# Transposing on the tensor engine instead of by DMA in an attention block between two feed-forward halves

## The chip, the core and the metric

The kernel runs on one core of a Trainium2 chip. The metric is device time in microseconds (us) of one execution of the whole program. Five engines work side by side, each through its own in-order queue: PE (matrix multiplication), DVE (vector), ACT (activation functions and copies), POOL (general) and SP, which here only issues DMAs. SBUF is the on-chip memory that all of them read; PE writes its results to PSUM, whose banks hold 512 32-bit or 1024 16-bit numbers for each of 128 partitions.

## The reference

The input is `(2, 1024, 1024)` in 32-bit floats: two sequences of 1024 tokens, width 1024.

```
x = x + 0.5 * ffn(layernorm(x))
x = x + attention(layernorm(x))
x = x + 0.5 * ffn(layernorm(x))
```

- `ffn(y) = y @ base_w.T + base_b + 2 * sum over the top 2 of 8 experts of weight * (y @ A_e.T) @ B_e`, the experts being adapters of rank 16, with a softmax over the two best gate logits.
- `attention`: 32 query heads in 8 groups of 4 that share a key and value head, head width 32, rotary positions on queries and keys, causal mask, softmax, output projection.

## The kernel before

Tokens are worked in 16 tiles of 128 (`t`); a tile goes through the stages `a1` (first layer norm and feed-forward), `a2` (second layer norm's result times the key/value and query weights, rotary), attention, `c1` (output projection and third layer norm) and `c2` (second feed-forward). Every large product is made of three 16-bit products, high x high, high x low and low x high, so each left operand is kept as a high and a low half and must lie with its columns on the partitions, that is, transposed, in a tile `tt` of 2 x 8 blocks of 128 x 128.

Transposition happens in three places.

1. Behind each layer norm (`layernorm`, 48 in all). `Split.add` makes the high half on ACT (L329) and the low half on DVE (L330) into `hl`, and a DMA transposition on SP's queue (L333) turns both into `tt`. For the first layer norm of the first three tiles (`turn=t < NTURN`) `turn_rows` transposes the 32-bit rows on PE instead (L365) and splits them from PSUM (L367, L368).
2. Keys (`kv_out`, L548): the staged keys `kst`, 8 groups of 128 columns (three parts of 32 and the rows for maxima), are turned by one DMA into `kts`.
3. Queries (`qt_load`, L625): two head groups at a time are turned by one DMA from `qst` into a tile `qt`.

Attention of a tile and a head group goes in two passes. `unit_s1` multiplies queries and keys (L645, four matmuls of 128 columns to a bank of the pool `p_s1`, which has three), and DVE takes the row maxima (L662; on the diagonal block after ACT's copy L656 and POOL's mask L657, in tiles with more than two key blocks). The maxima have to enter the second pass as extra rows of the queries. In tiles with up to three key blocks (`L <= MPE`) PE turns them (`turn_maxima`, L692) and DVE spreads them into the query tile (L694); in the others they are written into `qst` and the queries are turned again with them by a second DMA (L682, L683, then `qt_load`). `unit_s2` multiplies keys and queries (L796, one matmul of 512 columns), ACT takes the exponential (L802), and `av_batch` multiplies with values and ones (L739) after DVE's pair sums (L718).

The order is written out by hand. Attention units run along in a fixed order, first passes some units ahead of second passes (`look`, `LOOK`); between two steps of a second pass `step` takes pieces of dense work (`chunks`) from the list that `plan` gives for that tile, a few steps behind (`behind`). The program's scheduler then orders each engine's instructions. The weights of `a2` and `c1` do not fit in SBUF and are streamed: `prefetch` (L416) puts a load of 1 MB on SP's queue as soon as one of three buffers is free. Stores of results (L832, L834) and loads of `x` (L142) are on SP's queue too, in program order with the transpositions. One tile, `LATE`, is parked in DRAM (`xlate`, `qlate`) and taken up last.

Of the kernel before, what the change touches and what calls it, by code (L numbers as in the profile page):

```python
# [9 lines left out]
FP = mybir.dt.float32  # L10
# [24 lines left out]
LOFF = 2  # L35
MPE = 3
NTURN = 3
SB, LB = 3, 2
# [3 lines left out]
def kernel(  # L42
# [76 lines left out]
    qst = [stat.tile([P, NH, P], HP, name=f"qst{j}") for j in range(2)]  # L119
    ksts = [stat.tile([P, NKV, P], HP, name=f"kst{j}") for j in range(2)]  # L120
    kts = stat.tile([P, TPB + 1, NKV, P], HP)
    wss = [stat.tile([P, 2, KB // 2, 512], HP, name=f"ws{j}") for j in range(3)]
    for kst in ksts:
        nc.gpsimd.memset(kst[:, :, MR : MR + MC], -MROW)
        nc.gpsimd.memset(kst[:, :, MR + MC :], 0.0)
    mms = stat.tile([P, MR + MC], HP, name="mm")
    nc.gpsimd.memset(mms, 0.0)

# [25 lines left out]
    S, INV = {}, {}  # L154
    stream = deque()
    stage_ctx = ExitStack()
    stg = stage_ctx.enter_context(tc.tile_pool(name="stg", bufs=1))
# [135 lines left out]
    def prep_rest():  # L293
        yield from prep_stream(2, (0, 1), [(1, 0, 0), (1, 1, 1)], True)
        yield from prep_stream(3, (2, 3), [(4, 0, 2), (4, 1, 5)], False)
        yield from prep_stream(0, (2, 0), [None, None], True)
        for j in range(2):
            nc.gpsimd.memset(qst[j][:, :, 3 * DH :], 0.0)
        yield from prep_stream(1, (1, 2), [None, None], True)
        yield from prep_stream(4, (0, 1), [None, None], False)  # L300
# [14 lines left out]

    class Split:


        def __init__(self, n):
            self.hl = hlp.tile([P, 2 * D], HP, name="hl")  # L320
            self.tt = tp.tile([P, 2 * KB, P], HP, name="tt")
            self.n, self.done = n, 0

        def add(self, src):

            w, i = D // self.n, self.done
            src = src[:, i * w : (i + 1) * w]
            hi = self.hl[:, 2 * i * w : (2 * i + 1) * w]
            nc.scalar.copy(hi, src)  # L329
            nc.vector.tensor_tensor(self.hl[:, (2 * i + 1) * w : (2 * i + 2) * w], src, hi, ALU.subtract)  # L330
            m = 2 * KB // self.n
            pin(
                nc.sync.dma_start_transpose(  # L333
                    out=self.tt[:, i * m : (i + 1) * m, :], in_=self.hl[:, 2 * i * w : (2 * i + 2) * w]
                )
            )
            self.done += 1

        def high(self, k):
            m = KB // self.n  # L340
            return self.tt[:, k // m * 2 * m + k % m, :]

        def low(self, k):
            m = KB // self.n
            return self.tt[:, k // m * 2 * m + m + k % m, :]

    class Halves:


        def __init__(self):  # L350
            self.tt = tp.tile([P, 2 * KB, P], HP, name="tt")

        def high(self, k):
            return self.tt[:, k, :]

        def low(self, k):
            return self.tt[:, KB + k, :]

    def turn_rows(xn):
# [10 lines left out]

    def layernorm(xt, n=1, turn=False):
        st = small.tile([P, 2, 6], FP, name="bst")
        for c in range(2):
            nc.vector.bn_stats(st[:, c, :], xt[:, bass.ts(c, 512)])  # L374
        mv = small.tile([P, 2], FP, name="mv")
        nc.vector.bn_aggr(mv, st.rearrange("p a b -> p (a b)"))
        ve = small.tile([P, 1], FP, name="ve")
        nc.gpsimd.tensor_scalar(ve, mv[:, 1:2], EPS, None, ALU.add)
        r = small.tile([P, 1], FP, name="r")
        nc.gpsimd.tensor_tensor(r, ve, mhalf, ALU.pow)  # L380
        n1 = small.tile([P, 1], FP, name="n1")
        nc.vector.scalar_tensor_tensor(n1, ve, r, r, ALU.mult, ALU.mult)
        nc.vector.tensor_scalar(n1, n1, -0.5 * XS, 1.5 * XS, ALU.mult, ALU.add)
        rs = small.tile([P, 1], FP, name="rs")
        nc.vector.tensor_tensor(rs, n1, r, ALU.mult)
        nb = small.tile([P, 1], FP, name="nb")
        nc.vector.scalar_tensor_tensor(nb, mv[:, 0:1], -1.0, rs, ALU.mult, ALU.mult)
        xn = fpool.tile([P, D], FP, name="xn")
        if turn:
            nc.scalar.activation(xn, xt, AF.Identity, bias=nb, scale=rs)  # L390
            return turn_rows(xn)
        sp = Split(n)
        for i in range(n):
            c = bass.ts(i, D // n)
            nc.scalar.activation(xn[:, c], xt[:, c], AF.Identity, bias=nb, scale=rs)
            sp.add(xn)
        return sp

    def dense(ps, tt, wsel, n=512, last=True):

        for k in range(KB):
            wh, wl = wsel(k)
            th, tl = tt.high(k), tt.low(k)
            nc.tensor.matmul(ps, lhsT=th, rhs=wh, start=(k == 0), stop=False)  # L404
            nc.tensor.matmul(ps, lhsT=th, rhs=wl, start=False, stop=False)  # L405
            nc.tensor.matmul(ps, lhsT=tl, rhs=wh, start=False, stop=(last and k == KB - 1))  # L406
            if k % 2 == 1:
                yield
# [87 lines left out]
    def stage_a1(t):  # L496
# [3 lines left out]
        def done(n):  # L500
            if n == 1:
                Ts["x2", t] = layernorm(xts[t])
                if t == LATE:
                    late["x"] = dram.tile([P, D], FP, name="xlate")
                    nc.sync.dma_start(out=late["x"], in_=xts.pop(t))
# [29 lines left out]
    def kv_out(t, ps):  # L535
# [11 lines left out]
        kt = kts[:, (t + TPB) % (TPB + 1)]  # L547
        nc.sync.dma_start_transpose(out=kt, in_=ks.rearrange("p g c -> p (g c)"))  # L548
        KT[t] = kt

    def q_out(t, n, ps):
# [7 lines left out]
        if t == LATE and n == 1:  # L559
            late["q"] = dram.tile([P, NH, P], HP, name="qlate")  # L560
            nc.sync.dma_start(out=late["q"], in_=qs)

# [11 lines left out]
    def stage_a2x(t):  # L574

        ts = (t, t + 1)
        tts = [Ts.pop(("x2", u)) for u in ts]
        for ci in (2, 0, 1):
            pss = [p_dense.tile([P, 512], FP, name="pd") for u in ts]
# [19 lines left out]
    def first_a2(ts):  # L599

        tts = [Ts.pop(("x2", t)) for t in ts]
        for ci in (2, 0, 1):
            pss = [p_dense.tile([P, 512], FP, name="pd") for t in ts]
# [17 lines left out]
    def qt_load(t, g):  # L621

        assert ready[t] == 2 or g * GRP < NH // 2
        q = qtp.tile([P, 2 * GRP, P], HP, name="qt")
        nc.sync.dma_start_transpose(  # L625
            out=q, in_=QS[t][:, g * GRP : (g + 2) * GRP, :].rearrange("p h c -> p (h c)")
        )
        return q

    def unit_s1(t, g):  # L630
# [4 lines left out]
        if not odd:  # L635
            Ts["mx"] = small.tile([P, 2, TPB, GRP], FP, name="mx", bufs=2)
        mx = Ts["mx"]
        q = Ts["q1", (t, g - odd)][:, odd * GRP : (odd + 1) * GRP, :]
        for j in reversed(range(L)):
# [23 lines left out]
            if turned:  # L663
                turn_maxima()
            yield
# [6 lines left out]
        else:  # L672
            m = mx[:, :, 0, :]
        if L <= MPE:
            mm = mms[:, MR:].rearrange("p (i a h) -> p i a h", i=2, a=2)
            nc.vector.tensor_scalar(mm[:, 0], m, 1.0 / MROW, None, ALU.mult)
            nc.vector.scalar_tensor_tensor(mm[:, 1], m, 1.0 / MROW, mm[:, 0], ALU.mult, ALU.subtract)
            turned.append((t, g - 1, q1))
            return
        qs = QS[t][:, (g - 1) * GRP : (g + 1) * GRP].rearrange("p (a h) c -> p a h c", a=2)  # L680
        mh, ml = qs[:, :, :, 3 * DH], qs[:, :, :, 3 * DH + 1]
        nc.vector.tensor_scalar(mh, m, 1.0 / MROW, None, ALU.mult)  # L682
        nc.vector.scalar_tensor_tensor(ml, m, 1.0 / MROW, mh, ALU.mult, ALU.subtract)  # L683
        Ts["q2", t, g - 1] = qt_load(t, g - 1)

    turned = deque()

    def turn_maxima():

        t, g, q1 = turned.popleft()  # L690
        ps = p_s1.tile([P, GRP, P], FP, name="s1")[:, 0, :]
        nc.tensor.matmul(ps[0 : MR + MC], lhsT=mms, rhs=ident16, start=True, stop=True)  # L692
        rows, heads = slice(MR, MR + MC), [MC, 2 * GRP, P]
# [92 lines left out]
    def unit_s2(t, g):  # L786
# [7 lines left out]
        for j in range(L):  # L794
            ps = p_s2.tile([P, GRP, P], FP, name="s2")
            ins = nc.tensor.matmul(  # L796
                ps.rearrange("p h k -> p (h k)"), lhsT=KT[b0 + j][:, g, :],
                rhs=q.rearrange("p h k -> p (h k)"), start=True, stop=True,
            )
# [3 lines left out]
            if j == L - 1:  # L803
# [3 lines left out]
                )  # L807
            av_add(t, g, j, L, p32)
            yield

# [102 lines left out]
    for t in START:  # L913
        if t == "f":
# [4 lines left out]
            continue  # L919
        for _ in chunk(a1[t]):  # L920
            if len(stream) < 3:
                next(pr, None)
# [6 lines left out]

    qtp = ctx.enter_context(tc.tile_pool(name="qt", bufs=5, reuse_waits="tile"))  # L930
    pp = ctx.enter_context(tc.tile_pool(name="pp", bufs=2, reuse_waits="tile"))
# [85 lines left out]
    def step(s):  # L1017
# [28 lines left out]
        for g in range(NKV):  # L1046
# [3 lines left out]
            if s == NT - 1 and g == 3:  # L1050
                QS[LATE] = qst[LATE % 2]
                nc.sync.dma_start(out=QS[LATE], in_=late["q"])
            if u < len(units) and units[u][0] != t and s < NT - 1:
# [85 lines left out]
```

## Time and profile before

| | |
|---|---|
| median of 3 runs | 1512.1 us (1508.58 to 1515.14) |
| profiled execution: time, span | 1510.2 us, 1508.5 us |
| mean granted clock of PE | 0.978 |
| PE busy | 1407.3 us, 93% of the span |
| DVE, ACT, POOL busy | 1136.9, 749.4, 388.6 us |
| DMA | 269.40 MB in 265266 packets, 227472 of them under 512 B |
| DMA transpositions: layer norms, queries, keys | 45, 104, 16; median from issue to landing 6.1, 3.5, 5.6 us |

Busy time is time in which at least one instruction of the engine ran. A matmul's row shows its whole passage through the array, so that neighbours overlap: two matmuls of 512 columns, 0.38 us each, start 0.215 us apart. What one costs in a row of many is read from start to start. The granted clock is the share of full speed that the chip gave PE.

### The profile page before, as it was taken

The page shows a single profiled execution, that of the slowest core. Times are in us where ns is not written, and L with a number is a line of the kernel's source. Part 1 is how long each engine was busy: PE and PEld are TensorE (multiplying, and loading weights), DVE is VectorE, ACT ScalarE, POOL GpSimd, SP SyncE. Part 2 cuts the span into 40 slices and gives each one's busy share as a digit, 9 for nine tenths or more (in the row PEclk, how much of TensorE's full clock was granted, in tenths as well). Part 3 has the DMA queues.
Part 4 walks back from the last instruction along what each step waited for, and adds up shares of the span by engine and source line. Part 5 has one row for each costly group of instructions (what it writes and reads, how often), then busy time and mean ns, then how long its engine had stood idle before and what let it go on. Part 6 is the DMA issues. An engine that isn't in the chain of part 4 may idle for free.

```text
span 1508.5 us, 35338 instructions
## 1 busy us (share of the span) xinstructions
PE 1407.3 (93%) x14596; PEld 787.6 (52%) x14596; DVE 1136.9 (75%) x2411; ACT 749.4 (50%) x1356; POOL 388.6 (26%) x642
## 2 busy tenths in 40 slices
PE   5877889989999999999999898999999999989998
PEld 3333445545555555565654454555555556556544
DVE  6876957777869789688863687886869689789753
ACT  8563435444545455465561334553645456556531
POOL 3442224222322222222120133322322122221120
PEclk9998999999999999999999899999999999999999
DMA  8989187468487874846658858669595863923552
GB/s 294 324 193 245 24 214 192 141 166 261 90 285 87 237 186 85 258 114 141 192 145 269 181 185 239 188 162 264 105 297 78 242 162 87 275 82 86 127 163 76
DMA packets 265266, 269.40 MB, mean 179 GB/s; under 512 B 227472, under 2 KB 230544, under 8 KB 245392
## 3 DMA queue, kind: packets, MB, share of 16 engines
q1 hardware_dynamic: 259024, 239.87, 57.3%
q0 software_dynamic: 4640, 16.78, 6.5%
q10 hardware_dynamic: 1440, 10.49, 1.9%
q8 instruction: 114, 1.87, 0.5%
q14 instruction: 48, 0.39, 0.1%
HBM read 191.60 MB, written 20.45 MB: 141 GB/s over the span
## 4 chain that ended last, share of the span: by engine, by line
PE 68%; DVE 13%; DMA 10%; ACT 3%; issue 3%; POOL 1%; SPq 1%; ACTq 0%; DVEq 0%; POOLq 0%
PE pd L404 13%; PE pd L405 13%; PE pd L406 13%; PE av L739 11%; PE s L796 6%; PE s L645 6%; DMA ws<-wstr 4%; DVE mx L662 4%; DMA tt<-hl 3%; DVE pair L718 2%; DMA qt<-qst 1%; DVE o L748 1%; ACT p L802 1%; DVE bst L374 1%; PE pd L487 1%
## 5 line engine op out<-in xcount | busy, mean ns | idle before, releaser
L802 ACT ACTIVATE p<-s,cs 128x512 f32<-128x512 f32 x576 | 380.8, 688 | 266.9 <-PE s L796 260.4
L662 DVE TENSOR_REDUCE mx<-s 128x4 f32<-128x512 f32 x480 | 315.5, 675 | 55.7 <-PE s L645 45.4
L718 DVE TENSOR_TENSOR pair<-p,p 128x512 f32<-128x512 f32 x256 | 178.0, 697 | 62.3 <-ACT p L802 30.9
L645 PE MATMUL s<-kts,qt 96*128 96x128 f16 x2304 | 217.9, 221 | 7.1 <-DVE mx L662 2.6
L796 PE MATMUL s<-qt,kts 128*128 128x512 f16 x576 | 211.0, 385 | 11.8 <-ACT p L802 5.8
L404 PE MATMUL pd<-ws,tt 128*128 128x512 f16 x544 | 208.8, 384 | 14.1 <-DMA ws<-wstr 11.5
L645 PEld LDWEIGHTS <-qt 96*128 96x128 f16 x2304 | 165.4, 99 | 100.7 <-issue 30.1
L405 PE MATMUL pd<-ws,tt 128*128 128x512 f16 x544 | 208.2, 383 | 0.0
L406 PE MATMUL pd<-ws,tt 128*128 128x512 f16 x544 | 207.3, 382 | 0.0
L404 PE MATMUL pd<-wb,tt 128*128 128x512 f16 x512 | 197.9, 387 | 8.5 <-DVE xt L491 5.0
L404 PEld LDWEIGHTS <-tt 128*128 128x128 f16 x1312 | 130.5, 99 | 139.3 <-DMA tt<-hl 14.9
L405 PE MATMUL pd<-wb,tt 128*128 128x512 f16 x512 | 197.1, 385 | 1.4 <-DVE wb L213 1.4
L405 PEld LDWEIGHTS <-tt 128*128 128x128 f16 x1312 | 130.8, 100 | 128.7 <-issue 24.2
L406 PE MATMUL pd<-wb,tt 128*128 128x512 f16 x512 | 197.1, 385 | 0.0
L406 PEld LDWEIGHTS <-tt 128*128 128x128 f16 x1312 | 130.5, 100 | 125.0 <-issue 10.6
L739 PE MATMUL av<-p,va 128*32 128x128 f32 x4608 | 166.9, 278 | 4.6 <-ACT o L746 2.6
L804 POOL TENSOR_SCALAR_AFFINE_SELECT p<-p 128x512 f32<-128x512 f32 x128 | 90.7, 712 | 234.9 <-ACT p L802 228.3
L739 PEld LDWEIGHTS av<-p,va 128*32 128x32 f32 x4608 | 115.6, 110 | 68.1 <-issue 52.9
L755 POOL TENSOR_TENSOR tt<-o,tt 128x128 f16<-128x128 f32 x128 | 66.6, 521 | 325.9 <-ACT tt L754 325.8
L748 DVE RECIPROCAL o<-o 128x128 f32<-128x128 f32 x128 | 120.8, 944 | 21.4 <-ACT o L746 21.2
L657 POOL TENSOR_SCALAR_AFFINE_SELECT sm<-sm 128x512 f32<-128x512 f32 x96 | 66.2, 689 | 203.1 <-ACT sm L656 198.0
L754 ACT CAST tt<-o 128x128 f16<-128x128 f32 x128 | 38.0, 297 | 110.0 <-DVE o L753 105.8
(203 smaller groups left out, 1891.1 us busy)
## 6 DMA issues: line engine op xcount, KB each, us to landing
ws<-wstr SPq DMA_DIRECT2D x142, 1024.0 KB, 5.8
xt<-hb POOLq DMA_DIRECT2D x32, 512.0 KB, 6.3
wstr<-ws ACTq DMA_DIRECT2D x9, 1024.0 KB, 6.1
xt<-in_x_dram SPq DMA_DIRECT2D x16, 512.0 KB, 3.9
out_dram<-xt SPq DMA_DIRECT2D x15, 512.0 KB, 2.9
ws<-in_wb_dram SPq DMA_DIRECT2D x2, 1024.0 KB, 8.7
qst<-in_wb_dram SPq DMA_DIRECT2D x2, 1024.0 KB, 13.2
st<-in_wo_dram SPq DMA_DIRECT2D x2, 1024.0 KB, 14.4
```

What stands on the lines that cost most here:

```text
L404: nc.tensor.matmul(ps, lhsT=th, rhs=wh, start=(k == 0), stop=False)
L405: nc.tensor.matmul(ps, lhsT=th, rhs=wl, start=False, stop=False)
L406: nc.tensor.matmul(ps, lhsT=tl, rhs=wh, start=False, stop=(last and k == KB - 1))
L645: nc.tensor.matmul(ps[:, h, :], lhsT=q[0 : 3 * DH, h, :], rhs=KT[b0 + j][0 : 3 * DH, g, :], start=(not pem or h == 0), stop=not pem,)
L662: nc.vector.tensor_reduce(mx[:, odd, j, :], ps, AX.X, ALU.max)
L718: nc.vector.tensor_tensor(sums, us[i][1], us[i + 1][1], ALU.add)
L739: prev = nc.tensor.matmul(av[rows, i, :], lhsT=w, rhs=p32[:, h, :], start=(us[0][0] == 0 and n == 0), stop=(last and n == len(runs) - 1), ...
L748: nc.vector.reciprocal(rc, rc)
L755: nc.gpsimd.tensor_tensor(c.low(g), o2, c.high(g), ALU.subtract)
L796: ins = nc.tensor.matmul(ps.rearrange("p h k -> p (h k)"), lhsT=KT[b0 + j][:, g, :], rhs=q.rearrange("p h k -> p (h k)"), start=True, stop ...
L802: nc.scalar.activation(p32, ps, AF.Exp, scale=cs)
L804: nc.gpsimd.affine_select(out=p32, in_=p32, compare_op=ALU.is_ge, fill=0.0, base=0, pattern=[[0, GRP], [1, P]], channel_multiplier=-1,)
```

## The change

All 165 DMA transpositions are replaced by transposes on PE.

- `turned8` takes a bank of `p_s1`, transposes eight 16-bit blocks into it and lets ACT copy the 1024 columns out.
- Layer norms: `turn_halves` makes both halves as before, and puts their transposes into a queue, `later`. They are issued `TLAG` = 8 and 9 ticks afterwards, a tick being a step of `unit_s2` (or a piece of dense work in the start), or at once by `settle` when a dense stage is about to read the tile. The second layer norm of the first three tiles (`NTURN2`) goes by `turn_rows` in 32 bits.
- Keys and queries go by `turned8` in place.
- Maxima go by `turn_maxima` in all tiles, `MLAG` = 2 further blocks after the pair that they belong to, with two staging tiles `mm` in turn. The second turning of queries is gone.
- Key and query tiles use 112 rows where they used 128, `qlate` 96 columns of 128, and the unused columns are not zeroed any more.

```diff
-    class Split:
-        def __init__(self, n):
-            self.hl = hlp.tile([P, 2 * D], HP, name="hl")
-            self.tt = tp.tile([P, 2 * KB, P], HP, name="tt")
...
-        def add(self, src):
...
-            nc.scalar.copy(hi, src)
-            nc.vector.tensor_tensor(self.hl[:, (2 * i + 1) * w : (2 * i + 2) * w], src, hi, ALU.subtract)
-            m = 2 * KB // self.n
-            pin(
-                nc.sync.dma_start_transpose(
-                    out=self.tt[:, i * m : (i + 1) * m, :], in_=self.hl[:, 2 * i * w : (2 * i + 2) * w]
-                )
-            )
...
     class Halves:
         def __init__(self):
             self.tt = tp.tile([P, 2 * KB, P], HP, name="tt")
+            self.todo = 0
+
+        def settle(self):
+            while self.todo:
+                do_later()
...
+    def turned8(out, src, rows):
+        ps = p_s1.tile([P, GRP, P], FP, name="s1").rearrange("p h k -> p (h k)").bitcast(HP)
+        ps = ps.rearrange("p (b q) -> p b q", q=P)
+        for b in range(8):
+            nc.tensor.transpose(ps[0:rows, b, :], src[:, b, 0:rows], ident16)
+        nc.scalar.copy(out, ps[0:rows])
+
+    later = deque()
+
+    def do_later():
+        later.popleft()[1]()
+
+    def tick():
+        for n, entry in enumerate(later):
+            entry[0] -= 1
+        if later and later[0][0] <= 0:
+            do_later()
+
+    def turn_halves(xn):
+        c = Halves()
+        hl = hlp.tile([P, 2 * KB, P], HP, name="hl")
+        for n in range(2):
+            h = hl[:, n * KB : (n + 1) * KB, :]
+            hi = hl[:, 0:KB, :].rearrange("p k c -> p (k c)")
+            if n == 0:
+                nc.scalar.copy(hi, xn)
+            else:
+                nc.vector.tensor_tensor(h.rearrange("p k c -> p (k c)"), xn, hi, ALU.subtract)
+
+            def turn(n=n, h=h):
+                turned8(c.tt[:, n * KB : (n + 1) * KB, :], h, P)
+                c.todo -= 1
+
+            c.todo += 1
+            later.append([TLAG + n, turn])
+        return c
...
     def dense(ps, tt, wsel, n=512, last=True):
+        tt.settle()
...
-                Ts["x2", t] = layernorm(xts[t])
+                Ts["x2", t] = layernorm(xts[t], turn=t < NTURN2)
...
-        nc.sync.dma_start_transpose(out=kt, in_=ks.rearrange("p g c -> p (g c)"))
+        turned8(kt[0 : MR + MC], ks, MR + MC)
...
-            late["q"] = dram.tile([P, NH, P], HP, name="qlate")
-            nc.sync.dma_start(out=late["q"], in_=qs)
+            late["q"] = dram.tile([P, NH, MR], HP, name="qlate")
+            nc.sync.dma_start(out=late["q"], in_=qs[:, :, 0:MR])
...
         q = qtp.tile([P, 2 * GRP, P], HP, name="qt")
-        nc.sync.dma_start_transpose(
-            out=q, in_=QS[t][:, g * GRP : (g + 2) * GRP, :].rearrange("p h c -> p (h c)")
-        )
+        turned8(q[0:MR], QS[t][:, g * GRP : (g + 2) * GRP, :], MR)
         return q
...
             if turned:
-                turn_maxima()
+                turned[0][3] -= 1
+                if turned[0][3] < 0:
+                    turn_maxima()
...
-        if L <= MPE:
-            mm = mms[:, MR:].rearrange("p (i a h) -> p i a h", i=2, a=2)
-            nc.vector.tensor_scalar(mm[:, 0], m, 1.0 / MROW, None, ALU.mult)
-            nc.vector.scalar_tensor_tensor(mm[:, 1], m, 1.0 / MROW, mm[:, 0], ALU.mult, ALU.subtract)
-            turned.append((t, g - 1, q1))
-            return
-        qs = QS[t][:, (g - 1) * GRP : (g + 1) * GRP].rearrange("p (a h) c -> p a h c", a=2)
-        mh, ml = qs[:, :, :, 3 * DH], qs[:, :, :, 3 * DH + 1]
-        nc.vector.tensor_scalar(mh, m, 1.0 / MROW, None, ALU.mult)
-        nc.vector.scalar_tensor_tensor(ml, m, 1.0 / MROW, mh, ALU.mult, ALU.subtract)
-        Ts["q2", t, g - 1] = qt_load(t, g - 1)
+        while len(turned) > 1:
+            turn_maxima()
+        mm = mms[g // 2 % 2][:, MR:].rearrange("p (i a h) -> p i a h", i=2, a=2)
+        nc.vector.tensor_scalar(mm[:, 0], m, 1.0 / MROW, None, ALU.mult)
+        nc.vector.scalar_tensor_tensor(mm[:, 1], m, 1.0 / MROW, mm[:, 0], ALU.mult, ALU.subtract)
+        turned.append([t, g - 1, q1, MLAG])
...
             av_add(t, g, j, L, p32)
+            tick()
             yield
```

More of the change, by code (lines that the diff above doesn't have):

```diff
@@ L35 @@
 LOFF = 2
-MPE = 3
-NTURN = 3
+NTURN, NTURN2 = 3, 3
+MLAG = 2
+TLAG = 8
 SB, LB = 3, 2
@@ L119 @@
     qst = [stat.tile([P, NH, P], HP, name=f"qst{j}") for j in range(2)]
-    ksts = [stat.tile([P, NKV, P], HP, name=f"kst{j}") for j in range(2)]
+    ksts = [stat.tile([P, NKV, MR + MC], HP, name=f"kst{j}") for j in range(2)]
     kts = stat.tile([P, TPB + 1, NKV, P], HP)
@@ L124 @@
         nc.gpsimd.memset(kst[:, :, MR : MR + MC], -MROW)
-        nc.gpsimd.memset(kst[:, :, MR + MC :], 0.0)
-    mms = stat.tile([P, MR + MC], HP, name="mm")
-    nc.gpsimd.memset(mms, 0.0)
+    mms = [stat.tile([P, MR + MC], HP, name=f"mm{j}") for j in range(2)]
+    for mm in mms:
+        nc.gpsimd.memset(mm, 0.0)
     xts, Ts = {}, {}
@@ L155 @@
     stream = deque()
+    qtp = ctx.enter_context(tc.tile_pool(name="qt", bufs=5, reuse_waits="tile"))
     stage_ctx = ExitStack()
@@ L296, in prep_rest @@
         yield from prep_stream(0, (2, 0), [None, None], True)
-        for j in range(2):
-            nc.gpsimd.memset(qst[j][:, :, 3 * DH :], 0.0)
         yield from prep_stream(1, (1, 2), [None, None], True)
@@ L313, in scales @@
             S["uo", n] = u
-    class Split:
-        def __init__(self, n):
-            self.hl = hlp.tile([P, 2 * D], HP, name="hl")
-            self.tt = tp.tile([P, 2 * KB, P], HP, name="tt")
-            self.n, self.done = n, 0
-        def add(self, src):
[L326 to L329, printed above, removed]
-            nc.vector.tensor_tensor(self.hl[:, (2 * i + 1) * w : (2 * i + 2) * w], src, hi, ALU.subtract)
-            m = 2 * KB // self.n
-            pin(
-                nc.sync.dma_start_transpose(
-                    out=self.tt[:, i * m : (i + 1) * m, :], in_=self.hl[:, 2 * i * w : (2 * i + 2) * w]
-                )
-            )
[L337 to L345, printed above, removed]
     class Halves:
@@ L369, in turn_rows, with layernorm @@
         return c
-    def layernorm(xt, n=1, turn=False):
+    def layernorm(xt, turn=False):
         st = small.tile([P, 2, 6], FP, name="bst")
@@ L388, in layernorm @@
         xn = fpool.tile([P, D], FP, name="xn")
[L389 to L397, printed above, removed]
+        nc.scalar.activation(xn, xt, AF.Identity, bias=nb, scale=rs)
+        return turn_rows(xn) if turn else turn_halves(xn)
     def dense(ps, tt, wsel, n=512, last=True):
+        tt.settle()
         for k in range(KB):
@@ L577, in stage_a2x @@
         tts = [Ts.pop(("x2", u)) for u in ts]
+        for tt in tts:
+            tt.settle()
         for ci in (2, 0, 1):
@@ L601, in first_a2 @@
         tts = [Ts.pop(("x2", t)) for t in ts]
+        for tt in tts:
+            tt.settle()
         for ci in (2, 0, 1):
@@ L635, in unit_s1 @@
         if not odd:
-            Ts["mx"] = small.tile([P, 2, TPB, GRP], FP, name="mx", bufs=2)
+            Ts["mx"] = small.tile([P, 2, TPB, GRP], FP, name="mx", bufs=1)
         mx = Ts["mx"]
@@ L673, in unit_s1 @@
             m = mx[:, :, 0, :]
-        if L <= MPE:
-            mm = mms[:, MR:].rearrange("p (i a h) -> p i a h", i=2, a=2)
-            nc.vector.tensor_scalar(mm[:, 0], m, 1.0 / MROW, None, ALU.mult)
-            nc.vector.scalar_tensor_tensor(mm[:, 1], m, 1.0 / MROW, mm[:, 0], ALU.mult, ALU.subtract)
-            turned.append((t, g - 1, q1))
-            return
-        qs = QS[t][:, (g - 1) * GRP : (g + 1) * GRP].rearrange("p (a h) c -> p a h c", a=2)
-        mh, ml = qs[:, :, :, 3 * DH], qs[:, :, :, 3 * DH + 1]
-        nc.vector.tensor_scalar(mh, m, 1.0 / MROW, None, ALU.mult)
-        nc.vector.scalar_tensor_tensor(ml, m, 1.0 / MROW, mh, ALU.mult, ALU.subtract)
-        Ts["q2", t, g - 1] = qt_load(t, g - 1)
+        while len(turned) > 1:
[4 more added lines that the diff above has]
+        turned.append([t, g - 1, q1, MLAG])
     turned = deque()
     def turn_maxima():
-        t, g, q1 = turned.popleft()
+        t, g, q1, _ = turned.popleft()
         ps = p_s1.tile([P, GRP, P], FP, name="s1")[:, 0, :]
-        nc.tensor.matmul(ps[0 : MR + MC], lhsT=mms, rhs=ident16, start=True, stop=True)
+        nc.tensor.matmul(ps[0 : MR + MC], lhsT=mms[g // 2 % 2], rhs=ident16, start=True, stop=True)
         rows, heads = slice(MR, MR + MC), [MC, 2 * GRP, P]
@@ L796, in unit_s2 @@
             ins = nc.tensor.matmul(
-                ps.rearrange("p h k -> p (h k)"), lhsT=KT[b0 + j][:, g, :],
-                rhs=q.rearrange("p h k -> p (h k)"), start=True, stop=True,
+                ps.rearrange("p h k -> p (h k)"), lhsT=KT[b0 + j][0 : MR + MC, g, :],
+                rhs=q[0 : MR + MC].rearrange("p h k -> p (h k)"), start=True, stop=True,
             )
@@ L920 @@
         for _ in chunk(a1[t]):
+            tick()
             if len(stream) < 3:
@@ L928 @@
     stage_ctx.close()
-    qtp = ctx.enter_context(tc.tile_pool(name="qt", bufs=5, reuse_waits="tile"))
     pp = ctx.enter_context(tc.tile_pool(name="pp", bufs=2, reuse_waits="tile"))
@@ L1051, in step @@
                 QS[LATE] = qst[LATE % 2]
-                nc.sync.dma_start(out=QS[LATE], in_=late["q"])
+                nc.sync.dma_start(out=QS[LATE][:, :, 0:MR], in_=late["q"])
             if u < len(units) and units[u][0] != t and s < NT - 1:
```

## The prediction

> **What bounds the kernel now.** I read the busy table first, then the chain of waits by engine, then busy time by stretch, then what the tensor engine waits for, and last its timeline, to get prices. The first two:
>
> ```profile
> PE 1407.3 (93%) x14596; PEld 787.6 (52%) x14596; DVE 1136.9 (75%) x2411; ACT 749.4 (50%) x1356; POOL 388.6 (26%) x642
> PE 68%; DVE 13%; DMA 10%; ACT 3%; issue 3%; POOL 1%; SPq 1%; ACTq 0%; DVEq 0%; POOLq 0%
> ```
>
> PE shows 101.2 us without a matmul in a span of 1508.5, and no other engine is near it. Where these 101 us lie:
>
> ```profile
> 0.00:400.00 400.00, 338.54 (x2782) 180.50 (x2783) 299.60 (x671) 202.39 (x353) 126.38 (x222) 0.95 0.71 197
> 400.00:800.00 400.00, 394.16 (x4667) 229.13 (x4666) 313.23 (x643) 212.68 (x384) 94.02 (x148) 1.00 0.67 173
> ...
> 1000.00:1300.00 300.00, 294.82 (x3302) 168.76 (x3301) 233.15 (x486) 155.68 (x287) 76.36 (x120) 1.00 0.72 191
> ```
>
> The columns are PE, PE's weight loads, DVE, ACT and POOL, then granted clock, DMA share, GB/s. In the first 400 us, where weights arrive and are prepared, PE lacks 61 us; in the 700 us of the other two rows it lacks 11. Over all of 400 to 1508 us PE is busy for 1068.8 of 1108 us, 96%: there is little hole to put new PE work into. What PE waits for, as far as DMA goes:
>
> ```profile
> PE pd L404 <- DMA tt<-hl: 12.5, 6, 3.6
> PE pd L404 <- DMA ws<-wstr: 11.5, 10, 3.2
> PE s L796 <- DMA qt<-qst: 4.8, 5, 1.7
> PE s L645 <- DMA qt<-qst: 2.5, 2, 1.6
> ```
>
> (total, times, longest). All 165 DMA transpositions together cost PE 12.5 + 4.8 + 2.5 = 19.8 us, though the chain gives DMA 10%: while a transposition is on the chain, PE has other queued work. The prices come from the timeline and the groups:
>
> ```profile
> 901.68 0.61 PE L645 MATMUL s<-kts,qt 96*128 96x128 f16 x8
> 902.13 0.38 PE L404 MATMUL pd<-wb,tt 128*128 128x512 f16 x1
> ...
> 38.65 1.04 PE L365 MATMUL s<-ident,xn 128*128 128x128 f32 x8
> 39.52 0.39 PE L190 MATMUL s<-ident,sq 128*128 128x128 f32 x2
> ...
> 907.99 0.26 PE L692 MATMUL s<-ident,mm 128*112 128x128 f16 x1
> 908.09 0.61 PE L645 MATMUL s<-kts,qt 96*128 96x128 f16 x8
> ...
> L329 ACT CAST hl<-xn 128x1024 f16<-128x1024 f32 x45 | 46.9, 1043 | 2.6 <-DMA tt<-hl 2.2
> L656 ACT COPY sm<-s 128x512 f32<-128x512 f32 x96 | 56.1, 585 | 71.0 <-PE s L645 67.5 <-DVE qst L556 2.6 <-DVE mx L662 0.4
> L557 ACT CAST qst<-t 128x512 f16<-128x512 f32 x32 | 19.7, 615 | 0.0
> L694 DVE TENSOR_TENSOR qt<-s,picks 16x1024 f16<-16x1024 f32 x24 | 29.5, 1230 | 7.8 <-PE s L692 7.2
> ```
>
> A matmul's own duration holds its pipeline, so I price from start to start: eight 16-bit matmuls of 128 columns, each with a weight load of its own, take 0.45 us (901.68 to 902.13), or 56 ns each. Eight 32-bit transposes take 0.87 us, 109 each. A turned maxima matmul takes 0.10.
>
> **The change part by part.** Counts are those of the changed program's instruction list.
>
> PE work added. Of 48 layer norms, 3 went by PE in 32 bits and 45 by DMA; now 6 and 42. 42 + 16 key tiles x 8 + 64 pairs of head groups x 8 = 672 + 128 + 512 = 1312 16-bit transposes, by 56 ns = 73 us. No row of before is a 16-bit transpose; the nearest is L645, a 16-bit matmul of as many columns with as many loads. The L692 load of 112 columns took 134 ns against 99 for 128, which could touch the 640 transposes of keys and queries. Lower end 56; upper end 109, the 32-bit transpose's price: 143 us. I take 56. Three more layer norms go by 32-bit transposes: 24 x 0.109 = 2.6. Maxima by PE in all 64 pairs, not 24: 40 x 0.10 = 4. Together 80 us.
>
> Here a rule speaks against the change much more strongly. The Trainium skill, "TensorE: Matmul & The Clock Gate", Part 4: PE-mode transpose, gives about 275 ns for one 128x128 bf16 transpose in a kernel's context, and says that transposes do not count as PE activity for the clock. By it the 1312 would cost 361 us, and the result would lie near 1,880. Such a figure looks like a duration with latency: L692 has 251 ns in its group and 0.10 us from start to start. I take the row's 56; the clock is at 1.00 from 400 to 800 us, and a group of eight lasts only 0.45 us.
>
> Interruptions on PE. In the changed order PE's stream has 191 more changes from one source line to another (2287 against 2096). Pricing all matmuls of before by start to start (4256 of 512 columns at 0.2155 us, 2304 of L645 at 0.0555, 768 of 136 columns at 0.058, 7168 of L739 at 0.0275, 76 others at about 0.11) gives 1295 us, so some 215 of the 1508.5 are not issue; 86 of these are waits that the list of waits names, 129 are spread over 2096 changes, 0.06 each at most. 191 x 0.05 = 10 (0 to 20).
>
> ACT work added. 84 + 16 + 64 = 164 copies of 1024 elements out of a score bank. L656 has 585 ns for 512 elements from PSUM; L329 less L557 is 428 for 512 more; estimate 1.01 us each, 166 us. ACT goes from 749 to about 915 us, 58% of the new span: not a bound. But it is one in-order queue, and what waits behind each copy is the L802 exponential that the next L796 and the sums wait for.
>
> New waits. Transposed halves used to need a DMA of median 6.1 us from issue to landing; now transposes, then a copy, about 1.0 us plus what stands ahead on ACT (one L802, 0.69). In the changed PE order 30-odd of the 84 half groups have their first reader less than 1.7 us of matmul time behind them (the call that settles them stands just ahead of the dense stage); their missing time sums to 26 us, and 5 of the 16 key groups lack another 4. Queries stand nearly all 5 us or more ahead. Some of it lies in existing holes, some copies are later: 25 (10 to 60). PE's in-order stream stands behind each such wait, and behind it the next scores, exponentials and context sums.
>
> Score banks. 164 + 6 + 40 more tiles rotate through three banks; a bank under a copy is gone for about 2 us. Today L645 waits 2.6 us for a bank. By that row it is 1, by one copy each 164; near to the row, since a score tile comes only every 2.3 us: 8 (0 to 40).
>
> DVE. 40 more L694, 40 x 1.23 = 49 us, and six L368 (0.68) against three L330 (1.29): 1137 to 1186. It lies beside PE, which grows more; what waits for it is L796, with the maxima three or more units ahead. 0, and if the lead is gone, 40 x 1.23 at most.
>
> What goes. The 19.8 us of PE waits for transpositions. On SP's queue the 165 transpositions (1.2 to 1.9 us of issue each, some waiting tens of us for DVE) stood ahead of weight loads L416, stores L834 and loads L142; now those go first. Weight waits are 11.5 us; I take half. Together 26 (20 to 33). The LATE tile's parked queries go as pieces of 192 bytes, 4096 of them, on SP's queue instead of whole rows: landing was 4.7 to 6.4 us, a 512 KB transposition of small packets 6.1. With weight loads behind them 0 to 6; I take 0, hidden by the units ahead. POOL loses three memsets: nothing.
>
> Absorbed: about a quarter of the new PE work falls before 400 us, where 15% of PE is free: 10 (0 to 30).
>
> Sum against the profiled execution, 1510.2 us (span 1508.5 and 1.7 around it): 80 + 10 + 25 + 8 - 26 - 10 = 87, so 1597. The shown median of 1512.1 is 1.9 above that execution; I keep 1597. About 0.5% (8 us) is what a measurement of this kernel can tell from no change.
>
> **The rivals.**
>
> *Mostly absorbed.* If the copies land in time (25 and 8 become 5) and 30 us hide in the first 400 us: 80 + 10 + 5 - 33 - 30 = 32, so 1542. For: ACT is half idle, and PE's hidden gaps are 215 us. Against: the short leads counted above. Chance 0.15.
>
> *Faster: DMA sets the end.* The chain lists L404's tt<-hl at 3.3%, qt<-qst at 1.5% and ws<-wstr at 4.4%, 139 us in all. If the chain is literally what sets the end, freeing SP's queue takes these out: 1510 - 139 + 80 = 1451. It decides from the point at which more than about 80 us of PE's holes close, i.e. most of its 101 shown idle us. Against: PE waits for DMA only some 33 us, and from 400 us on it is busy for 96%. Chance 0.06.
>
> *Transposes dear, or ACT in the way.* At 109 ns each, 70 us more: 1667. Or each of 164 copies delays an exponential for which PE stands: 164 x 0.4 = 66 more, 1663. For: in-order queues, and L796 has two banks. Against: 56 ns in L645, ACT at 58%. Chance 0.16.
>
> That the change does not do what it says is excluded: SP's list holds no transposition any more.
>
> **How the numbers follow.** Likeliest (1560 to 1635): 0.60. Absorbed: 0.15. Dear: 0.16. Faster by over 0.5%: 0.06. Within 0.5%: 0.03, the thin end of the absorbed case. Slower: 0.91. The range takes the likeliest and most of the absorbed and dear cases, 1530 to 1660, leaving out the faster case and the far ends.
>
> **What would show it.** In the new profile: DMA_TRANSPOSE gone, packets under 512 B down from 227472 by most; eight transposes on one line about 0.45 us from start to start; their copies near 1.0 us, ACT near 915, DVE near 1186 and PE at 93% or more of a longer span; waits of L404's successor for the new copy in place of tt<-hl. Wrong if PE's share falls below 90% with waits on ACT leading (the dear case), or if the stretch from 400 us on takes no longer than before.

## The result and the profile after

The changed kernel takes 1605.5 us (median, 1604.76 to 1606.15) against 1511.7 for the kernel before (now four runs): a ratio of 1.062, interval 1.0596 to 1.0644. It is 94 us slower. The profiled execution took 1606.15 us, with a span of 1604.4.

First the lines of the new page that answer to those of before: the busy table, and the DMA packets.

```profile
PE 1496.2 (93%) x15972; PEld 872.6 (54%) x15972; DVE 1190.8 (74%) x2454; ACT 895.8 (56%) x1523; POOL 383.3 (24%) x639
...
DMA packets 52890, 213.96 MB, mean 133 GB/s; under 512 B 15344, under 2 KB 18416, under 8 KB 33264
```

PE has 1376 more matmuls and is again busy for 93%, now of a longer span. DMA moves 212 thousand packets fewer, and the kernel is slower all the same. The chain that ended last cannot be compared: the new page follows it over only 16% of the span.

Busy time by stretch (PE, PE's weight loads, DVE, ACT, POOL, then clock, DMA share, GB/s):

```profile
0.00:400.00 400.00, 352.71 (x3114) 200.42 (x3115) 301.27 (x667) 237.72 (x393) 127.37 (x218) 0.96 0.48 162
400.00:800.00 400.00, 385.57 (x4615) 231.46 (x4614) 313.30 (x619) 232.42 (x397) 85.37 (x138) 0.98 0.38 127
```

In the first 400 us PE fits 332 more matmuls into the same time. In the next 400 us it fits 52 fewer than before, and lacks 14 us where it lacked 6. To see where the time is lost I took the start of each tile's last exponential in both traces:

| last exponential of tile | before, us | after, us | difference |
|---|---|---|---|
| (first exponential of all) | 142.9 | 133.4 | -9.5 |
| 3 | 386.2 | 385.2 | -1.0 |
| 5 | 574.1 | 587.2 | +13.1 |
| 7 | 783.3 | 820.9 | +37.6 |
| 11 | 1065.5 | 1125.1 | +59.6 |
| 15 | 1433.1 | 1524.7 | +91.6 |

Up to tile 3 the change is free. All of it is paid from there on, where PE had few holes.

The prices, from the timeline of after (start, duration, what) and its groups:

```profile
302.16 0.62 PE L339 MATMUL s<-ident,hl 128*128 128x128 f16 x8
302.62 0.38 PE L804 MATMUL s<-qt,kts 112*128 112x512 f16 x1
```

```profile
L340 ACT COPY tt<-s 128x1024 f16<-128x1024 f16 x84 | 84.3, 1017 | 44.8 <-PE s L339 44.3
...
L339 PE MATMUL s<-ident,hl 128*128 128x128 f16 x672 | 53.5, 225 | 3.1 <-DVE mx L673 1.8 <-ACT qt L340 0.4 <-DVE qt L702 0.3
```

Eight transposes take 0.46 us from start to start (302.16 to 302.62), though each row shows 225 ns. A copy takes 1.02 us. And what PE waits for now (total, times, longest):

```profile
PE s L339 <- DVE qst L565: 11.9, 3, 4.6
PE s L656 <- DVE mx L673: 10.2, 15, 2.8
...
PE av L747 <- DVE pair L726: 8.9, 11, 2.6
PE s L656 <- DVE qt L702: 7.0, 9, 1.6
...
PE pd L413 <- DMA ws<-wstr: 4.5, 4, 1.5
...
PE s L339 <- DVE mx L673: 3.0, 6, 0.7
...
PE pd L413 <- ACT tt L340: 2.2, 3, 1.2
```

No wait for `tt<-hl` or `qt<-qst` is left, and the weight waits fell from 11.5 to 4.5 us. At the head stands a wait that before did not have: the transposes (L339) themselves, three times, for the rotated queries.

To compare runs I split each profiled span in two. "Issue" is the sum over all matmuls at their price from start to start at full clock (512 columns 0.215 us, 128 columns in 16 bits 0.054, and so on). "Rest" is the span less that: waits, interruptions, half-clock time, the start and the end.

| profiled span | span | issue | rest | clock |
|---|---|---|---|---|
| before | 1508.5 | 1290.7 | 217.8 | 0.978 |
| after | 1604.4 | 1366.1 | 238.3 | 0.976 |

So 75.4 us of the 95.9 are more issue, and 20.5 more rest. The issue is counted and priced, not timed as such. Two parts of the rest can be read from a trace: PE's idle time (the span less PE's busy time: 101.2 us before, 108.2 after) and half-clock time (the stretches in which the trace's clock records have PE at half speed: 69 us before, 79 after). The experiments ask whether this reading holds.

### The profile page after: what moved, and what is told of

It reads as the page before. It is cut to its first block, busy times and chain, and to the rows that moved or that the text cites. A ratio compares the mean times of both kernels' runs of the same rounds, so it can differ in the third digit from the quotient of the medians.

```text
span 1604.4 us, 37830 instructions
## 1 busy us (share of the span) xinstructions
PE 1496.2 (93%) x15972; PEld 872.6 (54%) x15972; DVE 1190.8 (74%) x2454; ACT 895.8 (56%) x1523; POOL 383.3 (24%) x639
## 5 line engine op out<-in xcount | busy, mean ns | idle before, releaser
L673 DVE TENSOR_REDUCE mx<-s 128x4 f32<-128x512 f32 x480 | 315.4, 678 | 61.2 <-PE s L656 53.6
L656 PE MATMUL s<-kts,qt 96*128 96x128 f16 x2304 | 211.3, 223 | 20.4 <-DVE mx L673 10.2
L656 PEld LDWEIGHTS <-qt 96*128 96x128 f16 x2304 | 161.6, 99 | 97.3 <-issue 49.8
L804 PE MATMUL s<-qt,kts 112*128 112x512 f16 x576 | 205.3, 387 | 8.1 <-ACT p L810 5.3
L414 PEld LDWEIGHTS <-tt 128*128 128x128 f16 x1312 | 129.8, 99 | 131.1 <-issue 19.8
L413 PEld LDWEIGHTS <-tt 128*128 128x128 f16 x1312 | 129.7, 99 | 122.3 <-issue 11.5
L340 ACT COPY tt<-s 128x1024 f16<-128x1024 f16 x84 | 84.3, 1017 | 44.8 <-PE s L339 44.3
```

The costliest lines, as they stand in the source:

```text
L340: nc.scalar.copy(out, ps[0:rows])
L656: nc.tensor.matmul(ps[:, h, :], lhsT=q[0 : 3 * DH, h, :], rhs=KT[b0 + j][0 : 3 * DH, g, :], start=(not pem or h == 0), stop=not pem,)
L673: nc.vector.tensor_reduce(mx[:, odd, j, :], ps, AX.X, ALU.max)
L804: ins = nc.tensor.matmul(ps.rearrange("p h k -> p (h k)"), lhsT=KT[b0 + j][0 : MR + MC, g, :], rhs=q[0 : MR + MC].rearrange("p h k -> p (h ...
```

## Experiments

My theory was that PE's issue sets the end. The rivals were that latency does it (waits for copies and inputs), or ACT's queue, or DVE's spreads. All times are medians; ratios are to the kernel before, timed beside each group of runs, with their 95% intervals. The changed kernel was timed once, and the medians of the kernel before lay between 1508.9 and 1511.7, so a difference from 1605.5 is good to some 3 us. The program's scheduler lays out every variant anew, so an edit can also move instructions that it does not name.

**1. Every transpose twice** (`e1_transposes_twice`).

```diff
-        for b in range(8):
+        for b in list(range(8)) * 2:
             nc.tensor.transpose(ps[0:rows, b, :], src[:, b, 0:rows], ident16)
```

> Every turned8 issues its eight transposes twice into the same bank; nothing else changes. If PE's issue time sets the end (my theory), 1312 more transposes at 56 ns cost 73 us on top of 1605.5: 1670 to 1685 us. If the changed kernel is slow because of latency (waits for the copies or the inputs of the transposes), a group lasts only 0.45 us longer and most of that lies in the waits: under 1630.

Measured: 1641.3 us (1.0875, 1.0855 to 1.0894), 36 us more than the changed kernel. Neither number was met. Issue rose by 70.6 us as foreseen, to 1436.7, but the rest fell by 35, from 238.3 to 203.5. The busy table, and PE's wait for rotated queries (total, times, longest):

```profile
PE 1549.1 (94%) x17284; PEld 940.7 (57%) x17284; DVE 1194.9 (73%) x2454; ACT 897.3 (55%) x1523; POOL 378.8 (23%) x639
```

```profile
PE s L339 <- DVE qst L565: 7.1, 2, 3.6
```

With 1312 more matmuls PE is busy for 52.9 us more and waits less. The changed kernel therefore held some 35 us that its work does not require. About half of them are PE's idle time, 91.1 us here and 108.2 in the changed kernel. Most of the other half goes with half-clock time, 40 us here and 79 there. Why the order of this run has less of both is not seen from it.

**2. Every copy twice** (`e2_copies_twice`).

```diff
-        nc.scalar.copy(out, ps[0:rows])
+        for _ in range(2):
+            nc.scalar.copy(out, ps[0:rows])
```

> ACT makes each of the 164 copies out of the bank twice: 166 us more for ACT, nothing more for PE. PE theory: 1605 to 1625, the rest of ACT's load lies beside PE. Rival, that the copies stand in front of the exponentials for which PE waits: 0.4 us for each of 164, 66 more, 1671.

Measured: 1649.5 us (1.0929, 1.0903 to 1.0955), 44 more, between the two. The issue is the same 1366.1; the rest went from 238 to 285. From PE's waits (L811 is the exponential, L341 the copy):

```profile
PE s L805 <- ACT p L811: 12.9, 33, 1.6
...
PE pd L414 <- ACT tt L341: 5.6, 5, 2.5
...
PE s L339 <- ACT qt L341: 4.1, 2, 3.8
PE s L339 <- ACT tt L341: 3.5, 2, 3.0
```

The wait of the second pass for the exponential rose from 5.3 us to 12.9. The waits for the copies themselves, in all rows, rose more: from 5.3 us to about 20. A further copy costs 0.27 us of time for 1.02 us of ACT. ACT at 56% is not out of the way, as my sum had it.

**3 and 4. Halves, or queries, by DMA again** (`e3_halves_by_dma`, `e4_queries_by_dma`).

```diff
-                turned8(c.tt[:, n * KB : (n + 1) * KB, :], h, P)
...
+        nc.sync.dma_start_transpose(out=c.tt, in_=hl.rearrange("p k c -> p (k c)"))
```

> The changed kernel with the layer norms' halves turned by one DMA each again (42 of them); keys, queries and maxima stay on PE. PE theory: 672 transposes go, 38 us, and 4 us of interruptions, the 12.5 us of waits for these DMAs come back: about 1576. Rival, that the cost is one per group and copy (94 us over 164 groups): 84 x 0.57 = 48 less, 1557.

```diff
-        turned8(q[0:MR], QS[t][:, g * GRP : (g + 2) * GRP, :], MR)
+        nc.sync.dma_start_transpose(
+            out=q, in_=QS[t][:, g * GRP : (g + 2) * GRP, :].rearrange("p h c -> p (h c)")
+        )
```

> The changed kernel with the first turning of queries by DMA again (64 of them); halves, keys and maxima stay on PE. PE theory: 512 transposes go, 29 us; with them go the waits of these transposes for their inputs (12 on PE for DVE's qst, up to 10 more in the weight loads for ACT's), and 7 us of waits for query DMAs come back: 1605 - 29 - 15 + 7 = 1568. If those input waits only move elsewhere: 1582.

The edit of 4 also zeroes the unused columns of `qst` again, by two memsets on POOL in the start.

Measured: 1540.0 us (1.0203, 1.0185 to 1.0221) and 1539.1 us (1.0194, 1.0172 to 1.0215). Each removal gives 66 us, far more than either expectation. Their issue fell by only 36.2 and 27.6 us; the rest of it is 28.8 and 38.1 us of "rest". Two parts that give 66 each out of a total of 94 cannot be separate costs.

**5. Maxima by PE alone, in the kernel before** (`e5_maxima_on_pe`).

```diff
-MPE = 3
+MPE = 8
```

> The kernel before with maxima turned by PE in all 64 pairs (MPE = 8), nothing else changed: 40 turned matmuls (4 us of PE) and 40 spreads on DVE (49 us) more, 40 DMA transpositions fewer. PE theory: +4 and a few us of waits for the spreads, 1512 to 1522. Rival, that DVE's spreads are what made the changed kernel slow: 40 x 0.6 or more, over 1534.

Measured: 1527.0 us (1.0107, 1.0081 to 1.0134), between the two again: 16 us slower. The profiled execution was a quick one, with a span of 1520.9 us; in it 2 us more are issue and 10 more rest. PE's waits for spreads grew from 1.8 us to 6.4, for the pair sums from 1.7 to 7.9, and the matmul that turns the maxima (L692) now waits 11.3 us for its own input where it waited 5.3. Turning the maxima on PE costs, but not most of the 94. The run lacks `MLAG` and the second staging tile, which the changed kernel has.

**6. Early second norms alone, in the kernel before** (`e6_second_norms_early`).

```diff
-                Ts["x2", t] = layernorm(xts[t])
+                Ts["x2", t] = layernorm(xts[t], turn=t < NTURN2)
```

> The kernel before with the second layer norms of the first three tiles turned by PE in 32 bits (NTURN2 = 3), nothing else changed. The changed kernel began its exponentials 9.5 us earlier (133.4 against 142.9 us). If this comes from these three norms and is kept to the end: 1500 to 1504. Rival, that another wait takes the lead back: 1507 to 1512.

Measured: 1511.0 us (0.9999, 0.9976 to 1.0023): no change. At the end of tile 6 it is 6.8 us ahead, at the end of tile 15 2.7. Most of the lead is taken back.

**7. Halves and queries both by DMA** (`e7_keys_maxima_norms`), the edits of 3 and 4 together.

> The changed kernel with halves and queries both turned by DMA, so that only keys, maxima and the early second norms are on PE. If what the two removals gave (65.5 and 66.4 us, each alone) were their own costs, they add: 1605 - 132 = 1474. Theory: their issue adds (36 + 28 us), the rest of each (waits and half-clock windows, some 30 to 38) is mostly shared and can go only once: 1605 - 64 - 35 = 1506, between 1495 and 1512.

Measured: 1529.7 us (1.0137, 1.011 to 1.0163). That is above all that was expected, and it turns the question round. From 1530 on, turning the queries on PE adds 10 us (run 3), turning the halves adds 9 (run 4), and both add 76. The split shows where the time lies, with the two parts of the rest that a trace shows:

| | span | issue | rest | PE idle | half-clock time |
|---|---|---|---|---|---|
| 7: keys, maxima, norms on PE | 1532.5 | 1302.4 | 230.1 | 107.2 | 73.0 |
| 3: and queries | 1539.4 | 1329.9 | 209.5 | 94.2 | 31.5 |
| 4: and halves | 1538.7 | 1338.5 | 200.2 | 88.5 | 38.4 |
| after: all | 1604.4 | 1366.1 | 238.3 | 108.2 | 78.7 |

Each kind alone adds 28 or 36 us of issue, and most of it is made up again by less idle time and by half-clock time, which falls to about half. With both, neither is lower than in run 7, and the rest grows. So it is not that two kinds fill the same holes: with both, the holes are as large as without. Run 7 is itself a poor order, with nearly the rest of the changed kernel (its profiled execution was the slowest of four, 1534.2 us); some of the gap between 10 + 9 and 76 comes from that.

**8. Keys and early norms, in the kernel before** (`e8_keys_norms_early`): the edit of 6, and

```diff
-        nc.sync.dma_start_transpose(out=kt, in_=ks.rearrange("p g c -> p (g c)"))
+        turned8(kt, ks, P)
```

> The kernel before with keys turned by PE (128 transposes and 16 copies) and the early second norms in 32 bits; halves, queries and the maxima of longer tiles by DMA as before. Theory: 7 us of issue and at most 4 of copies against the early lead of 9: 1505 to 1515. If a key transposition by DMA (5.6 us to landing) sits on the way to the first scores of each tile: below 1500.

Measured: 1505.9 us (0.9976, 0.9957 to 0.9996), within the first expectation.

**9. Queries' transposes deferred** (`e9_queries_later`). The trace of after shows what such a wait is. From 916.8 us, the last matmul of the queries' dense stage, PE's stream goes straight to the transposes of the same queries, which have still to be rotated on ACT, DVE and POOL:

```profile
916.82 0.38 PE L415 MATMUL pd<-ws,tt 128*128 128x512 f16 x1
...
920.99 0.69 DVE L565 TENSOR_TENSOR qst<-t,qst 128x512 f16<-128x512 f32 x1 [0.68 <-ACT qst L564]
...
921.83 1.06 PE L339 MATMUL s<-ident,qst 128*96 128x128 f16 x8 [4.64 <-DVE qst L565]
...
923.11 0.63 PE L661 MATMUL s<-cmask,negid 128*128 128x512 f16 x1
...
923.54 1.91 PE L339 MATMUL s<-ident,hl 128*128 128x128 f16 x16
```

PE stands for 4.64 us, and everything queued behind stands with it. Then eight transposes take 0.85 us and a matmul of 512 columns 0.43: the clock is halved, as the stretches of 3 us say (PE first, granted clock third from the end):

```profile
917.00:920.00 3.00, 0.19 (x1) 0.00 (x0) 1.07 (x2) 1.09 (x2) 1.41 (x2) 1.00 0.75 224
920.00:923.00 3.00, 1.17 (x11) 1.20 (x12) 1.00 (x2) 1.21 (x3) 0.00 (x0) 0.53 0.46 194
923.00:926.00 3.00, 3.00 (x27) 2.63 (x26) 0.78 (x2) 2.30 (x4) 0.08 (x1) 0.50 0.00 0
926.00:929.00 3.00, 3.00 (x33) 2.24 (x32) 2.24 (x4) 1.44 (x4) 0.77 (x2) 0.83 0.00 0
```

The edit puts these transposes into the queue of deferred ones:

```diff
-        turned8(q[0:MR], QS[t][:, g * GRP : (g + 2) * GRP, :], MR)
+        src = QS[t][:, g * GRP : (g + 2) * GRP, :]
+        def turn():
+            turned8(q[0:MR], src, MR)
+            waiting.discard((t, g))
+        waiting.add((t, g))
...
+        later.insert(n, [QLAG, turn])
...
+        while (t, g - odd) in waiting:
+            do_later()
```

> The changed kernel with the transposes of queries put into the queue of deferred transposes, 4 ticks back, or issued when their scores are due. In the changed kernel three of them stood on PE for 11.9 us waiting for the rotated queries, 10.2 more in the weight loads, and half-clock windows followed. Theory (halves and queries together cost some 56 us more than each alone because transposes stand in PE's order ahead of their inputs): 1605 less 20 to 30 us, 1575 to 1585. Rival (score banks and copies are short with both kinds): 1598 to 1610.

Measured: 1573.8 us (1.0437, 1.0412 to 1.0462), 32 us faster than the changed kernel with the same instructions: issue 1366.1 as before, rest 205.7 instead of 238.3. In this run PE waits for those inputs 5.3 us in place of 11.9; all of PE's idle time is 91 us where it was 108, and half-clock time 51 where it was 79. The result lies 1 us below the theory's range and far from the rival's. The named wait itself gives back 6.6 of the 32 us; that the rest follows from it is likely, but the new order differs in other places too.

**10. TLAG 4 instead of 8** (`e10_tlag_4`).

> The changed kernel with TLAG 4 instead of 8: the same instructions, only the halves' transposes stand some 9 us earlier in the order. If the order of PE's stream is what makes the two kinds together dear, a shift like this moves the time by 15 us or more either way. If it is the amount of work on banks and ACT: 1600 to 1611.

Measured: 1624.2 us (1.0771, 1.0745 to 1.0797), 19 us slower with the same instructions; the rest is 254.6. The halves' transposes now stand in PE's order ahead of the cast that feeds them:

```profile
PE s L339 <- ACT hl L362: 19.1, 5, 5.4
```

Before the shift this wait was not on PE's list; PE's idle time grew to 121 us and half-clock time to 94. So the place of the transposes in PE's order moved the time by 32 us one way and 19 the other.

**11. Halves copied by DVE** (`e11_halves_copied_by_dve`).

```diff
-        nc.scalar.copy(out, ps[0:rows])
+        if dve:
+            nc.vector.tensor_copy(out, ps[0:rows])
+        else:
+            nc.scalar.copy(out, ps[0:rows])
```

> The changed kernel with the 84 halves' banks copied out by DVE instead of ACT. If ACT's queue (the copies standing ahead of exponentials) carries half of the cost, as the doubling of copies with 44 us suggests: 84/164 of 44, 22 less, 1583. If DVE, at 74%, is as much in the way: 1600 to 1630.

Measured: 1620.6 us (1.0748, 1.0722 to 1.0774), 15 slower. The DVE copy itself is shorter than ACT's, but it stands in one queue with the spreads of maxima, for which PE's first-pass matmuls now wait 19.3 us where they waited 7.0 (the copy's group, and the first line of PE's waits):

```profile
L341 DVE COPY tt<-s 128x1024 f16<-128x1024 f16 x84 | 56.3, 678 | 14.8 <-PE s L339 14.4
```

```profile
PE s L659 <- DVE qt L705: 19.3, 16, 3.2
```

**12. First four tiles on PE** (`e12_first_tiles_on_pe`): run 8, and queries and maxima by PE in tiles 0 to 3.

```diff
+        if t < EARLY:
+            turned8(q, QS[t][:, g * GRP : (g + 2) * GRP, :], P)
+            return q
...
-        if L <= MPE:
+        if L <= MPE or t < EARLY:
```

> A try at a version faster than both: the kernel before with keys and early second norms on PE (1505.9 as measured), and also queries and maxima of the first four tiles, where PE has holes. The kernel with halves by DMA was 15.6 us ahead of before at the end of tile 3, the one with keys and early norms 4.2. If the lead is kept: 1495. If later waits take it back: 1504 to 1508.

Measured: 1506.2 us (0.9984, 0.9971 to 0.9997). It is 12.2 us ahead at the end of tile 3, 5.9 at the end of tile 4, and 6.5 at the end of tile 15: the second expectation. Runs 8 and 12 beat both kernels, by a quarter of a per cent and less, and their intervals end just below 1.

## Why the prediction was right, and where its sum was off

1597 was predicted and 1605.5 measured. The likeliest case came: most of the loss, 75 of 96 us of span, is PE's added issue, by count and measured price. That issue alone does not set the end is shown by run 1, where 70.6 us of it cost 36, and by run 9, which is 32 us faster with the same issue. The steps, one by one:

- **PE's added work: 80 predicted, 75.4 counted** as issue. The step that the forecast rested on held: a 16-bit transpose costs what a matmul of 128 columns costs, 56 to 57 ns from start to start (the split counts 54; at 56 the issue is 78). At the 109 ns of the 32-bit transpose the same work would have been 70 us dearer. The figure of about 275 ns that stood against it is near what a row's duration says (225 ns), not what a row costs in a stream; run 1 added 1312 transposes and 36 us, not 361. Nor did a kernel of twice as many transposes get a lower clock: 0.989 against 0.976.
- **What goes: 26 predicted, 26.8 measured** (19.8 us of waits for transpositions, and 7.0 of the weight waits, which fell from 11.5 to 4.5).
- **Score banks: 8 predicted.** The waits for DVE's L673 grew from 2.6 us to 10.2 for the scores, and the transposes themselves wait 3.0 for it: 10.6 more.
- **Absorbed: 10 predicted, more measured.** In the first 350 us PE issues 20 us more than before, and at 385 us the kernel is not behind.
- **Waits for copies: 25 predicted, mis-sized.** PE's own waits for L340 in all its rows sum to 5.3 us. The short leads that I counted in the order did not become waits of that size: the copies were mostly done when PE came to them. Twice as many copies do make PE wait for them, about 20 us in run 2.
- **Interruptions: 10 predicted, not measured by themselves.** An estimate from the traces takes from the rest PE's idle time and what half clock costs (half-clock time less the idle time and the full-speed price of the matmuls in it). That leaves 88 us before and 98 after, but also 102 in run 3 with half as many transposes, so the agreement proves nothing. The price was read from a list of PE's waits that sums to 95.8 us, not 86; it stays under 0.06.
- **Missed: the wait of a transpose for its input.** The sum asked who waits for the transposes' results and never what the transposes wait for. They wait 11.9 us on PE for rotated queries, half-clock time grew by 10 us, and run 9 took 32 us back by moving them. In the kernel before, such waits stood on SP's queue: L625 waited there 29.7 us for DVE's rotated queries (L556), and PE waited 7.3 for the transposed ones.
- **DVE's spreads: 0 predicted.** Waits for them grew from 1.8 to 9.1 us, and run 5, with 40 more spreads and turned maxima and 40 DMA transpositions fewer, is 16 us slower. Waits for the pair sums grew from 1.7 to 8.9. No run takes the maxima off PE in the changed kernel.

So the two missed terms and the copies' oversized one nearly cancelled: the smaller terms together were 7 in the sum, and the rest grew by 20.5. That the number came within 9 us is in part luck.

The rivals: the dear transposes are excluded by run 1, and DMA as what sets the end by the result itself. "ACT in the way" holds in part: by run 2 it charges 0.27 us a copy, not 0.4. The absorbed case, at 1542, is within 3 us of what runs 3 and 4 took, each with one kind on PE, which is chance, since it was reckoned for both. It failed because with both kinds PE stands idle for no less time than before, and part of that is a bad order: with the better one of run 9 the rest is 206 us, beside 196 to 210 in runs 1, 3, 4, 8 and 12. I read these 200 us as about the floor of this program, above which the time follows the issue. That it is a floor is argued from six layouts, not shown. How much of run 2's 44 us the copies cost, and how much a new layout, stays open.

## What to carry to other kernels

Before moving work to an engine that is busy for 96% of a stretch, price it from start to start on that engine; the DMA waits that it removes can be read off that engine's list of waits, here they were 27 us against 75 of new issue. A step moved from a DMA queue into an in-order engine brings its own input wait with it: place it in that engine's order behind its input, not only ahead of its reader. Two edits that each cost little alone (10 and 9 us here) can cost much together (76), so try them together before adding up.

## What the hardware showed that I had not expected

- A wait of 4.64 us on PE was followed by half clock: the granted clock was 0.53, 0.50 and 0.83 in three stretches of 3 us from 920 us on, around and behind the end of the wait at 921.83, and eight transposes took 0.85 us instead of 0.46.
- DVE copied 1024 16-bit columns of 128 partitions from PSUM in 678 ns, ACT in 1017.
- Loads of 96 and 112 columns took 123 and 130 ns (median), loads of 128 columns 98, and still the transposes behind all of them were 55 to 56 ns apart at full clock.
